# Pairwise bilinear products on one core: rows regrouped by partition, 102 stores over a ring of three, one transposed-x buffer, W in ten half loads

## The chip, the cores and the metric

The kernel runs on one core of a Trainium2 chip. Times are device microseconds, as medians of several executions; the span on a profile's page, from the first to the last instruction, is about 1.8 us shorter. Each kernel was compared with runs of the kernel before on the same chip.

## The reference, cut to what matters

```python
B, F, D = 4096, 32, 64                        # x: (B, F, D), W: (496, D, D), all float32
i_idx, j_idx = np.triu_indices(F, k=1)        # 496 pairs i < j
vi, vj = x[:, i_idx, :], x[:, j_idx, :]
inter = jnp.einsum('bpd,pde->bpe', vi, W) * vj
return inter.reshape(B, -1)                   # (4096, 31744): 520 MB
```

The output is 520 MB, against 42 MB of input. Below, a "unit" is one pair: 64 output columns. One tile is 128 batch rows and 496 units.

## The kernel before: the parts that matter

Two rows i of the triangle, 2p and 2p+1, run together: their two 64-row matmuls fill two PSUM banks, and one "doubled" multiply on VectorE takes both through an access pattern with two runs.

```python
STORES = [[0, 1], [2, 3], [4, 5], [6, 7, 8], [9, 10, 11, 12, 13, 14, 15]]
RING = 28160                                   # 440 units
def runs(tl, a, b, n):                         # two runs of n columns, at a and at b
    ap = tl[:, a : a + n]
    return bass.AP(ap.tensor, ap.offset, [list(ap.ap[0]), [b - a, 2], list(ap.ap[1])])
...
for p in range(NPR):                           # 16 loads of W, both halves at once
    nc.sync.dma_start(out=wp, in_=w[:, woff[p] : woff[p] + width[2 * p]])
...
for s, group in enumerate(STORES):             # five stores to a tile
    if at + store_w[s] > RING: at = 0
    osb = ring[:, at : at + store_w[s]]
    ...
            nc.vector.tensor_tensor(           # never leaves its own store's stretch
                runs(osb, o[0], o[1], n[0]), runs(pm, 0, half, n[0]),
                runs(xt, xj[0], xj[1], n[0]), ALU.mult)
    nc.sync.dma_start(out=out[ts(t, P), o0 : o0 + store_w[s]], in_=osb)
```

Of the kernel before, what the change touches and what calls it, by code (L numbers as in the profile page):

```python
# [1 line left out]

# [6 lines left out]

F32 = mybir.dt.float32  # L10
ALU = mybir.AluOpType

P = 128
BANK = 512
BANKS = 8
CHUNK = BANK

STORES = [[0, 1], [2, 3], [4, 5], [6, 7, 8], [9, 10, 11, 12, 13, 14, 15]]
PREFETCH_AT = [5, 6]
RING = 28160  # L20


@with_exitstack
def pair_bilinear_kernel(
    ctx: ExitStack,
    tc: tile.TileContext,
    x: bass.AP,
    w: bass.AP,
    out: bass.AP,
    F: int,  # L30
    D: int,
):




















    nc = tc.nc
    B = x.shape[0]
    NT = B // P
    NPR = F // 2

    width = [(F - 1 - i) * D for i in range(F)]
    off = [sum(width[:i]) for i in range(F)]
    woff = [sum(width[0 : 2 * p : 2]) for p in range(NPR)]  # L60
    store_w = [sum(width[2 * p] + width[2 * p + 1] for p in g) for g in STORES]

    const = ctx.enter_context(tc.tile_pool(name="const", bufs=1))
    xtpool = ctx.enter_context(tc.tile_pool(name="xT", bufs=2))
    psum = ctx.enter_context(tc.tile_pool(name="ps", bufs=1, space=bass.MemoryType.PSUM))

    ident = const.tile([P, P], F32, tag="ident", name="ident")
    make_identity(nc, ident)

    def runs(tl, a, b, n):  # L70

        ap = tl[:, a : a + n]
        return bass.AP(ap.tensor, ap.offset, [list(ap.ap[0]), [b - a, 2], list(ap.ap[1])])


    xbuf = [const.tile([P, (F + 1) * D], F32, tag=f"x{b}", name=f"x{b}") for b in range(2)]
    for xb in xbuf:
        nc.gpsimd.memset(xb[:, F * D :], 0.0)  # L78

    def load_x(t):  # L80
        xt = xbuf[t % 2]
        nc.scalar.dma_start(out=xt[:, : F * D], in_=x[ts(t, P), :])
        return xt

    pring = psum.tile([P, BANKS * BANK], F32, tag="pring", name="pring")
    bank = 0

    def take_banks(n):

        nonlocal bank  # L90
        if bank + n > BANKS:
            bank = 0
        got = pring[:, bank * BANK : (bank + n) * BANK]
        bank = (bank + n) % BANKS
        return got

    def transpose_x(xT, t, xt, g):

        n = 2 * BANK // P
        pt = take_banks(2)  # L100
        for c in range(n):
            nc.tensor.transpose(pt[:, ts(c, P)], xt[:, ts(n * g + c, P)], ident)  # L102
        nc.scalar.copy(xT[:, ts(g, 2 * BANK)], pt)  # L103

    def new_xT(t):
        return xtpool.tile([P, NPR * P], F32, tag="xT", name=f"xT_{t}")

    ring = const.tile([P, RING], F32, tag="ring", name="ring")
    at = 0
    xs = {0: load_x(0)}  # L110

    w_sb = []
    for p in range(NPR):
        wp = const.tile([P, width[2 * p]], F32, tag=f"w{p}", name=f"w{p}")
        nc.sync.dma_start(out=wp, in_=w[:, woff[p] : woff[p] + width[2 * p]])
        w_sb.append(wp)

    xTs = {0: new_xT(0)}
    for g in range(2):
        transpose_x(xTs[0], 0, xs[0], g)  # L120

    for t in range(NT):
        xt, xT = xs.pop(t), xTs.pop(t)
        if t + 1 < NT:
            xs[t + 1] = load_x(t + 1)
        for s, group in enumerate(STORES):
            if at + store_w[s] > RING:
                at = 0
            osb = ring[:, at : at + store_w[s]]
            at += store_w[s]  # L130
            o0 = off[2 * group[0]]
            for p in group:
                if t + 1 < NT and p in PREFETCH_AT:
                    if t + 1 not in xTs:
                        xTs[t + 1] = new_xT(t + 1)
                    transpose_x(xTs[t + 1], t + 1, xs[t + 1], PREFETCH_AT.index(p))
                for c0 in range(0, width[2 * p], CHUNK):
                    n = [max(0, min(CHUNK, width[2 * p + h] - c0)) for h in range(2)]
                    half = -(-n[0] // BANK) * BANK
                    pm = take_banks(2 * half // BANK)  # L140
                    for b0 in range(0, n[0], BANK):
                        b1 = min(b0 + BANK, n[0])
                        for h in range(2):
                            if b0 < n[h]:
                                nc.tensor.matmul(  # L145
                                    pm[:, h * half + b0 : h * half + b1],
                                    xT[h * D : (h + 1) * D, ts(p, P)],
                                    w_sb[p][h * D : (h + 1) * D, c0 + b0 : c0 + b1],
                                    start=True,
                                    stop=True,  # L150
                                )
                    o = [off[2 * p + h] - o0 + c0 for h in range(2)]
                    xj = [(2 * p + h + 1) * D + c0 for h in range(2)]
                    if n[1] > half - BANK and o[1] + n[0] <= store_w[s]:
                        nc.vector.tensor_tensor(  # L155
                            runs(osb, o[0], o[1], n[0]),
                            runs(pm, 0, half, n[0]),
                            runs(xt, xj[0], xj[1], n[0]),
                            ALU.mult,
                        )  # L160
                    else:
                        for h in range(2):
                            if n[h]:
                                nc.vector.tensor_tensor(  # L164
                                    osb[:, o[h] : o[h] + n[h]],
                                    pm[:, h * half : h * half + n[h]],
                                    xt[:, xj[h] : xj[h] + n[h]],
                                    ALU.mult,
                                )
            nc.sync.dma_start(out=out[ts(t, P), o0 : o0 + store_w[s]], in_=osb)  # L170


# [33 lines left out]
```

## Time and profile before

| | before |
|---|---|
| median, range | 1339.8 us, 1339.71 to 1339.87 |
| DMA queues, sum of the shares | 98.9% of 16 engines |
| VectorE, TensorE busy | 90%, 85% |
| first store's first packet, last completion | 27.6 us, 1336.8 us |

The main groups of instructions on the page (line, engine, operation, operands, count; busy us and mean ns; idle before and what ended it), and two lines of the list of DMA issues (size of each, median us from issue to landing):

```profile
L155 DVE TENSOR_TENSOR ring<-pring,x 128x1024 f32<-128x1024 f32 (+3 forms) x1056 | 1115.8, 1102 | 115.3 <-DMA out_dram<-ring 55.9
L145 PE MATMUL pring<-w,xT 64*128 64x512 f32 (+4 forms) x4864 | 1077.5, 560 | 165.7 <-DVE ring L155 161.4
...
out_dram<-ring SPq DMA_DIRECT2D x32, 3776.0 KB, 21.9
...
x<-in_x_dram ACTq DMA_DIRECT2D x32, 1024.0 KB, 14.2
```

A store lands 22 us after its issue although 3.8 MB take about 9 us at the measured rate: there is always another store ahead of it in the queue. That backlog is what keeps the DMA engines busy.

### The profile page before, as it was taken

How to read it: one execution, taken by the hardware profiler on the slowest of the kernel's cores; microseconds unless marked ns; L12 is line 12 of the kernel's file. 1: busy time of each engine (PE TensorE's matmuls, PEld its weight loads, DVE VectorE, ACT ScalarE, POOL GpSimd, SP SyncE). 2: the span in 40 equal slices, each digit the busy share in tenths (PEclk: the TensorE clock that was granted, in tenths of full speed). 3: DMA queues.
4: the chain of work that ended last, by engine and by line, in shares of the span. 5: the costliest groups of instructions: out<-in, count | busy, mean ns of one | idle time of the engine just before them, and what ended most of it. 6: DMA issues, size and time to landing. Idle time of an engine off the chain costs nothing.

```text
span 1338.1 us, 13157 instructions
## 1 busy us (share of the span) xinstructions
PE 1142.4 (85%) x5376; PEld 511.0 (38%) x5376; DVE 1199.8 (90%) x1376; ACT 66.1 (5%) x65; POOL 0.9 (0%) x8
## 2 busy tenths in 40 slices
PE   7899788898988988988889888889788898988982
PEld 3344333343344433433333334434344333433431
DVE  6999899898899988999889989899898998998993
ACT  1000000000000000000000000000000000000000
POOL 0000000000000000000000000000000000000000
PEclk9999999999998999999999999999999999999996
DMA  9999999999999999999999999999999999999996
GB/s 393 427 430 433 431 427 435 424 428 432 430 430 428 424 425 430 421 429 430 416 427 415 428 433 403 429 422 423 430 418 411 431 417 432 411 424 432 422 424 272
DMA packets 30012, 562.89 MB, mean 421 GB/s; under 512 B 3456, under 2 KB 3840, under 8 KB 5376
## 3 DMA queue, kind: packets, MB, share of 16 engines
q1 hardware_dynamic: 25344, 528.49, 92.7%
q10 hardware_dynamic: 4608, 33.56, 6.0%
q8 instruction: 42, 0.69, 0.2%
q14 instruction: 18, 0.15, 0.0%
HBM read 41.94 MB, written 520.09 MB: 420 GB/s over the span
## 4 chain that ended last, share of the span: by engine, by line
DMA 41%; DVE 39%; PE 16%; issue 2%; DVEq 0%
DMA out_dram<-ring 41%; DVE ring L155 35%; PE pring L145 13%; DVE ring L164 4%; PE pring L102 3%; DMA x<-in_x_dram 1%; DVEq L155 0%; DVEq L164 0%
## 5 line engine op out<-in xcount | busy, mean ns | idle before, releaser
L155 DVE TENSOR_TENSOR ring<-pring,x 128x1024 f32<-128x1024 f32 (+3 forms) x1056 | 1115.8, 1102 | 115.3 <-DMA out_dram<-ring 55.9
L145 PE MATMUL pring<-w,xT 64*128 64x512 f32 (+4 forms) x4864 | 1077.5, 560 | 165.7 <-DVE ring L155 161.4
L145 PEld LDWEIGHTS pring<-w,xT 64*128 64x128 f32 x4864 | 452.5, 189 | 758.6 <-DVE ring L155 601.3
L103 ACT COPY xT<-pring 128x1024 f32<-128x1024 f32 x64 | 64.8, 1013 | 1193.8 <-PE pring L102 1193.8
L164 DVE TENSOR_TENSOR ring<-pring,x 128x64 f32<-128x64 f32 (+3 forms) x320 | 114.5, 383 | 3.7 <-DVE ring L155 0.5
L102 PE MATMUL pring<-ident,x 128*128 128x128 f32 x512 | 73.6, 290 | 8.5 <-DMA x<-in_x_dram 8.5
L102 PEld LDWEIGHTS pring<-ident,x 128*128 128x128 f32 x512 | 58.5, 147 | 46.9 <-issue 36.9
L103 ACT ACT_TABLE_LOAD x1 | 1.3, 1283 | 1.7 <-PEq L198 1.7
masks.py:199 POOL TENSOR_SCALAR_AFFINE_SELECT ident<-ident 128x128 f32<-128x128 f32 x1 | 0.3, 294 | 0.0
L78 POOL MEMSET x<- 128x64 f32 x2 | 0.2, 152 | 0.0
masks.py:197 POOL MEMSET ident<- 128x128 f32 x1 | 0.2, 205 | 0.3 <-POOLq L198 0.3
L198 POOL MEMSET const-bfloat16-1.0<- 128x1 bf16 x1 | 0.1, 102 | 0.0
L198 POOL MEMSET const-uint8-127<- 128x1 uint8 x1 | 0.1, 102 | 0.0
L198 POOL MEMSET const-float32-0.0<- 128x1 f32 x1 | 0.1, 99 | 0.2 <-issue 0.2
L198 POOL MEMSET const-float32-1.0<- 128x1 f32 x1 | 0.1, 99 | 0.0
## 6 DMA issues: line engine op xcount, KB each, us to landing
out_dram<-ring SPq DMA_DIRECT2D x32, 3776.0 KB, 21.9
out_dram<-ring SPq DMA_DIRECT2D x32, 3264.0 KB, 21.6
out_dram<-ring SPq DMA_DIRECT2D x32, 3168.0 KB, 22.4
out_dram<-ring SPq DMA_DIRECT2D x32, 2912.0 KB, 21.4
out_dram<-ring SPq DMA_DIRECT2D x32, 2752.0 KB, 22.0
x<-in_x_dram ACTq DMA_DIRECT2D x32, 1024.0 KB, 14.2
w<-in_w_dram SPq DMA_DIRECT2D x1, 992.0 KB, 7.5
w<-in_w_dram SPq DMA_DIRECT2D x1, 928.0 KB, 11.8
```

The costliest lines, as they stand in the source:

```text
L78: nc.gpsimd.memset(xb[:, F * D :], 0.0)
L102: nc.tensor.transpose(pt[:, ts(c, P)], xt[:, ts(n * g + c, P)], ident)
L103: nc.scalar.copy(xT[:, ts(g, 2 * BANK)], pt)
L145: nc.tensor.matmul(pm[:, h * half + b0 : h * half + b1], xT[h * D : (h + 1) * D, ts(p, P)], w_sb[p][h * D : (h + 1) * D, c0 + b0 : c0 + b1 ...
L155: nc.vector.tensor_tensor(runs(osb, o[0], o[1], n[0]), runs(pm, 0, half, n[0]), runs(xt, xj[0], xj[1], n[0]), ALU.mult,)
L164: nc.vector.tensor_tensor(osb[:, o[h] : o[h] + n[h]], pm[:, h * half : h * half + n[h]], xt[:, xj[h] : xj[h] + n[h]], ALU.mult,)
L198: nc = bacc.Bacc("TRN2", target_bir_lowering=False, num_devices=1)
```

## The change

Its intent: each partition takes 32 neighbouring batch rows, so that a partition's output is one contiguous run and stores need not end with a tile. 101 stores of 157 units and a short one go through a ring of three slots, so fewer and longer packets. One transposed-x buffer pays for the larger ring. W is stored without padding and loaded by halves of 64 partitions.

```diff
-STORES = [[0, 1], [2, 3], [4, 5], [6, 7, 8], [9, 10, 11, 12, 13, 14, 15]]
-RING = 28160
+LOADS = [[0], [1], [2, 3], [4, 5, 6], [7, 8, 9, 10, 11, 12, 13, 14, 15]]
+STORE = 157 * 64
+SLOTS = 3
 ... (x of a tile: x[t], repacked on the host; out: (128, 32 * 31744))
-        nc.sync.dma_start(out=wp, in_=w[:, woff[p] : woff[p] + width[2 * p]])
+    for g in LOADS:
+        for h in range(2):
+            nc.sync.dma_start(out=w_sb[h * D : (h + 1) * D, a:b], in_=w[h * D : (h + 1) * D, a:b])
 ... (xT: one buffer, halves rewritten at pairs 9 and 3)
+                q = [t * cols + off[2 * p + h] + c0 for h in range(2)]
+                if n[1] and in_one_store(q[0], n[0]) and in_one_store(q[1], n[0]):
+                    at = [v % (SLOTS * STORE) for v in q]
+                    nc.vector.tensor_tensor(
+                        runs(ring, at[0], at[1], n[0]), runs(pm, 0, BANK, n[0]),
+                        runs(xt, xj[0], xj[1], n[0]), ALU.mult)
+                else:                          # single multiplies, cut at a store's end
+                    for h in range(2):
+                        multiply(q[h], pm, h * BANK, xt, xj[h], n[h])
+                if done // STORE * STORE > stored:
+                    store_to(done // STORE * STORE)
```

More of the change, by code (lines that the diff above doesn't have):

```diff
@@ L16 @@
 CHUNK = BANK
-STORES = [[0, 1], [2, 3], [4, 5], [6, 7, 8], [9, 10, 11, 12, 13, 14, 15]]
-PREFETCH_AT = [5, 6]
-RING = 28160
+LOADS = [[0], [1], [2, 3], [4, 5, 6], [7, 8, 9, 10, 11, 12, 13, 14, 15]]
+FIRST_HALF_AT, SECOND_HALF_AT = 9, 3
+STORE = 157 * 64
+SLOTS = 3
 @with_exitstack
@@ L53, in pair_bilinear_kernel @@
     nc = tc.nc
-    B = x.shape[0]
-    NT = B // P
+    NT = x.shape[0]
     NPR = F // 2
@@ L59, in pair_bilinear_kernel @@
     off = [sum(width[:i]) for i in range(F)]
-    woff = [sum(width[0 : 2 * p : 2]) for p in range(NPR)]
-    store_w = [sum(width[2 * p] + width[2 * p + 1] for p in g) for g in STORES]
+    cols = sum(width)
+    woff = [sum(width[i % 2 : i : 2]) for i in range(F)]
     const = ctx.enter_context(tc.tile_pool(name="const", bufs=1))
-    xtpool = ctx.enter_context(tc.tile_pool(name="xT", bufs=2))
     psum = ctx.enter_context(tc.tile_pool(name="ps", bufs=1, space=bass.MemoryType.PSUM))
@@ L81, in load_x @@
         xt = xbuf[t % 2]
-        nc.scalar.dma_start(out=xt[:, : F * D], in_=x[ts(t, P), :])
+        nc.scalar.dma_start(out=xt[:, : F * D], in_=x[t])
         return xt
@@ L95, in take_banks, with transpose_x @@
         return got
-    def transpose_x(xT, t, xt, g):
+    xT = const.tile([P, NPR * P], F32, tag="xT", name="xT")
+    def transpose_x(xt, g):
         n = 2 * BANK // P
@@ L103, in transpose_x @@
         nc.scalar.copy(xT[:, ts(g, 2 * BANK)], pt)
-    def new_xT(t):
-        return xtpool.tile([P, NPR * P], F32, tag="xT", name=f"xT_{t}")
-    ring = const.tile([P, RING], F32, tag="ring", name="ring")
-    at = 0
-    xs = {0: load_x(0)}
-    w_sb = []
-    for p in range(NPR):
-        wp = const.tile([P, width[2 * p]], F32, tag=f"w{p}", name=f"w{p}")
-        nc.sync.dma_start(out=wp, in_=w[:, woff[p] : woff[p] + width[2 * p]])
-        w_sb.append(wp)
-    xTs = {0: new_xT(0)}
-    for g in range(2):
-        transpose_x(xTs[0], 0, xs[0], g)
+    ring = const.tile([P, SLOTS * STORE], F32, tag="ring", name="ring")
@@ new lines, in pair_bilinear_kernel, with store_to, in_one_store, multiply @@
+    stored = 0
+    def store_to(end):
+        nonlocal stored
+        at = stored % (SLOTS * STORE)
+        nc.sync.dma_start(out=out[:, stored:end], in_=ring[:, at : at + end - stored])
+        stored = end
+    def in_one_store(q, n):
+        return q // STORE == (q + n - 1) // STORE
+    def multiply(q, pm, c, xt, xj, n):
+        while n:
+            m = min(n, STORE - q % STORE)
+            at = q % (SLOTS * STORE)
+            nc.vector.tensor_tensor(
+                ring[:, at : at + m], pm[:, c : c + m], xt[:, xj : xj + m], ALU.mult
+            )
+            q, c, xj, n = q + m, c + m, xj + m, n - m
@@ L122, in pair_bilinear_kernel @@
+    xs = {0: load_x(0)}
+    w_sb = const.tile([P, woff[F - 2] + width[F - 2]], F32, tag="w", name="w")
+    for g in LOADS:
+        for h in range(2):
+            a = woff[2 * g[0] + h]
+            b = woff[2 * g[-1] + h] + width[2 * g[-1] + h]
+            if h and g is LOADS[-1]:
+                b += D
+            nc.sync.dma_start(
+                out=w_sb[h * D : (h + 1) * D, a:b], in_=w[h * D : (h + 1) * D, a:b]
+            )
+    transpose_x(xs[0], 0)
     for t in range(NT):
-        xt, xT = xs.pop(t), xTs.pop(t)
+        xt = xs.pop(t)
@@ L124, in pair_bilinear_kernel @@
         if t + 1 < NT:
             xs[t + 1] = load_x(t + 1)
-        for s, group in enumerate(STORES):
-            if at + store_w[s] > RING:
-                at = 0
-            osb = ring[:, at : at + store_w[s]]
-            at += store_w[s]
-            o0 = off[2 * group[0]]
-            for p in group:
-                if t + 1 < NT and p in PREFETCH_AT:
-                    if t + 1 not in xTs:
-                        xTs[t + 1] = new_xT(t + 1)
-                    transpose_x(xTs[t + 1], t + 1, xs[t + 1], PREFETCH_AT.index(p))
-                for c0 in range(0, width[2 * p], CHUNK):
-                    n = [max(0, min(CHUNK, width[2 * p + h] - c0)) for h in range(2)]
-                    half = -(-n[0] // BANK) * BANK
-                    pm = take_banks(2 * half // BANK)
-                    for b0 in range(0, n[0], BANK):
-                        b1 = min(b0 + BANK, n[0])
-                        for h in range(2):
-                            if b0 < n[h]:
-                                nc.tensor.matmul(
-                                    pm[:, h * half + b0 : h * half + b1],
-                                    xT[h * D : (h + 1) * D, ts(p, P)],
-                                    w_sb[p][h * D : (h + 1) * D, c0 + b0 : c0 + b1],
-                                    start=True,
-                                    stop=True,
-                                )
-                    o = [off[2 * p + h] - o0 + c0 for h in range(2)]
-                    xj = [(2 * p + h + 1) * D + c0 for h in range(2)]
-                    if n[1] > half - BANK and o[1] + n[0] <= store_w[s]:
-                        nc.vector.tensor_tensor(
-                            runs(osb, o[0], o[1], n[0]),
-                            runs(pm, 0, half, n[0]),
-                            runs(xt, xj[0], xj[1], n[0]),
-                            ALU.mult,
-                        )
-                    else:
-                        for h in range(2):
-                            if n[h]:
-                                nc.vector.tensor_tensor(
-                                    osb[:, o[h] : o[h] + n[h]],
-                                    pm[:, h * half : h * half + n[h]],
-                                    xt[:, xj[h] : xj[h] + n[h]],
-                                    ALU.mult,
-                                )
-            nc.sync.dma_start(out=out[ts(t, P), o0 : o0 + store_w[s]], in_=osb)
@@ new lines, in pair_bilinear_kernel @@
+        for p in range(NPR):
+            if p == SECOND_HALF_AT:
+                transpose_x(xt, 1)
+            if p == FIRST_HALF_AT and t + 1 < NT:
+                transpose_x(xs[t + 1], 0)
+            for c0 in range(0, width[2 * p], BANK):
+                n = [max(0, min(BANK, width[2 * p + h] - c0)) for h in range(2)]
+                pm = take_banks(2)
+                for h in range(2):
+                    if n[h]:
+                        a = woff[2 * p + h] + c0
+                        nc.tensor.matmul(
+                            pm[:, h * BANK : h * BANK + n[0]],
+                            xT[h * D : (h + 1) * D, ts(p, P)],
+                            w_sb[h * D : (h + 1) * D, a : a + n[0]],
+                            start=True,
+                            stop=True,
+                        )
+                q = [t * cols + off[2 * p + h] + c0 for h in range(2)]
+                xj = [(2 * p + h + 1) * D + c0 for h in range(2)]
+                if n[1] and in_one_store(q[0], n[0]) and in_one_store(q[1], n[0]):
+                    at = [v % (SLOTS * STORE) for v in q]
+                    nc.vector.tensor_tensor(
+                        runs(ring, at[0], at[1], n[0]),
+                        runs(pm, 0, BANK, n[0]),
+                        runs(xt, xj[0], xj[1], n[0]),
+                        ALU.mult,
+                    )
+                else:
+                    for h in range(2):
+                        multiply(q[h], pm, h * BANK, xt, xj[h], n[h])
+                done = q[0] + n[0] if c0 + BANK < width[2 * p] else q[1] + n[1]
+                if done // STORE * STORE > stored:
+                    store_to(done // STORE * STORE)
@@ L173 @@
+    if stored < NT * cols:
+        store_to(NT * cols)
 def kernel(r_inputs, L0_rec_W):
@@ L179 @@
     NP = L0_rec_W.shape[0]
-    x = np.ascontiguousarray(r_inputs).reshape(B, F * D)
+    NT = B // P
+    x = np.ascontiguousarray(r_inputs.reshape(P, NT, F * D).transpose(1, 0, 2))
     wt = np.transpose(L0_rec_W, (1, 0, 2))
@@ L185 @@
     first = [sum(n[:i]) for i in range(F)]
-    halves = [
-        np.concatenate(
-            [
-                np.pad(wt[:, first[i] : first[i] + n[i]], ((0, 0), (0, h), (0, 0)))
-                for i in range(h, F, 2)
-            ],
-            axis=1,
-        )
-        for h in range(2)
-    ]
-    w = np.ascontiguousarray(np.stack(halves)).reshape(2 * D, -1)
+    w = np.zeros((2, D, sum(n[0::2]), D), wt.dtype)
+    for h in range(2):
+        of_h = [wt[:, first[i] : first[i] + n[i]] for i in range(h, F, 2)]
+        w[h, :, : sum(n[h::2])] = np.concatenate(of_h, axis=1)
+    w = w.reshape(2 * D, -1)
     nc = bacc.Bacc("TRN2", target_bir_lowering=False, num_devices=1)
@@ L200 @@
     w_d = nc.dram_tensor("in_w_dram", w.shape, F32, kind="ExternalInput").ap()
-    o_d = nc.dram_tensor("out_0_dram", (B, NP * D), F32, kind="ExternalOutput").ap()
+    o_d = nc.dram_tensor("out_0_dram", (P, NT * NP * D), F32, kind="ExternalOutput").ap()
     with tile.TileContext(nc) as tc:
@@ L204 @@
     r = run_bass_kernel_spmd(nc, [{"in_x_dram": x, "in_w_dram": w}], core_ids=[0])
-    return r.results[0]["out_0_dram"]
+    return r.results[0]["out_0_dram"].reshape(B, NP * D)
```

## The prediction

> **What bounds the kernel now.** I read the head of the page first (engine shares, the slices), then the DMA queues, the chain that ended last, the waits of VectorE, and last the transfers stretch by stretch.
>
> ```profile
> PE 1142.4 (85%) x5376; PEld 511.0 (38%) x5376; DVE 1199.8 (90%) x1376; ACT 66.1 (5%) x65; POOL 0.9 (0%) x8
> ...
> DMA  9999999999999999999999999999999999999996
> ...
> DMA packets 30012, 562.89 MB, mean 421 GB/s; under 512 B 3456, under 2 KB 3840, under 8 KB 5376
> ...
> q1 hardware_dynamic: 25344, 528.49, 92.7%
> q10 hardware_dynamic: 4608, 33.56, 6.0%
> q8 instruction: 42, 0.69, 0.2%
> ...
> DMA 41%; DVE 39%; PE 16%; issue 2%; DVEq 0%
> ```
>
> VectorE is busy 90% of the span, but the sixteen DMA engines are busy in every slice but the last. The queue shares add up to 98.9%: 0.989 x 1338.1 = 1323 us of packets on the mean DMA engine. Nothing else comes near. The chain of waits gives VectorE 39% because it counts the work between two waits for a freed ring; that is no sign that VectorE is short. Its waits:
>
> ```profile
> DVE ring L155 <- DMA out_dram<-ring: 55.9, 35, 3.0
> DVE ring L155 <- PE pring L145: 30.7, 27, 12.9
> ```
>
> Thirty-five times it stands until a store has left the ring. It could work faster than the stores drain. By stretch (columns: PE, PEld, DVE, ACT, POOL, granted clock, DMA share, GB/s):
>
> ```profile
> 0.00:26.00 26.00, 16.73 (x76) 8.62 (x77) 12.90 (x14) 3.31 (x3) 0.88 (x8) 1.00 0.94 377
> 26.00:80.00 54.00, 49.46 (x244) 22.40 (x243) 52.59 (x61) 4.05 (x4) 0.00 (x0) 1.00 1.02 433
> 80.00:160.00 80.00, 70.11 (x340) 31.11 (x338) 74.59 (x86) 4.05 (x4) 0.00 (x0) 1.00 1.00 431
> 160.00:640.00 480.00, 415.02 (x1952) 187.04 (x1950) 438.50 (x504) 22.28 (x22) 0.00 (x0) 0.97 1.00 428
> 640.00:1280.00 640.00, 559.64 (x2640) 249.11 (x2640) 586.11 (x674) 32.41 (x32) 0.00 (x0) 0.97 0.99 422
> 1280.00:1320.00 40.00, 31.44 (x134) 12.74 (x132) 35.11 (x41) 0.00 (x0) 0.00 (x0) 0.94 0.98 417
> 1320.00:1326.00 6.00, 0.00 (x0) 0.00 (x0) 0.00 (x0) 0.00 (x0) 0.00 (x0) 0.50 1.02 436
> 1326.00:1338.00 12.00, 0.00 (x0) 0.00 (x0) 0.00 (x0) 0.00 (x0) 0.00 (x0) 0.50 0.06 26
> ```
>
> Two things are to be seen. The transfers run at 431 to 433 GB/s at first and at 422 later. And in the last 12 us the share is 0.06, one engine of sixteen. In the trace's packet records fifteen engines post their last completion between 1326.6 and 1326.9 us, the sixteenth at 1336.8. While the others run, that one's packets take 2 to 3% longer than the median (888 ns for 23,296 bytes against 865; alone at the end it also does 865). Nearly one sixteenth of all store packets are longer by such an amount. I read this as one slow DMA engine: by mid-run it is about 10 us behind, the ring holds the other fifteen to its pace, and its own sum of packets is what the time consists of. This reading from packet records is the least certain part of the diagnosis; the DMA bound itself is certain.
>
> [...]
>
> **The change part by part.**
> What a packet costs: medians are 309 ns for 8,192 bytes and 1119 ns for 30,208, so (1119 - 309) / 22,016 = 0.0368 ns per byte (27.2 bytes per ns) and 7.6 ns fixed. A completion packet is 9 ns.
>
> Stores. The bytes are the same, 520.09 MB. A row of a store was 21.5 to 29.5 KB, is now 157 x 256 = 40,192 bytes. Stores fall from 160 to 102, packets per engine at 8 each from 1280 to 816: 464 x 7.6 ns = 3.5 us, and 58 completions x 9 ns = 0.5 us. Together -4.0 us, on the path as each engine's packets are the path.
>
> Ring. Before, 440 units of 64 columns in which stores of 118, 102, 86, 99 and 91 wrapped with waste; now three slots of 157, 471 units. VectorE fills a slot in some 157/496 of its 37.5 us per tile (1199.8/32), 11.9 us, and the DMA drains one in 157/496 of 41 us, 13.0 us. When a slot comes free two others are still queued, 26 us of work, so the slow engine never starves. It doesn't starve now either, so this buys nothing unless the waits cost the slow engine something.
>
> W. 16 loads of 128 partitions become ten of 64, alternately lower and upper half. Bytes: 31,808 columns x 64 rows x 4 = 8.14 MB instead of 8.39; 0.25 MB / 16 / 27.2 = 0.6 us, and 88 fewer packets per engine (16 x 8 to 10 x 4) another 0.7: -1.3 us. [...]508.9 KB per engine goes at 13.6 bytes per ns, 37.4 us, not 18.7: +18.7 us. These loads lie ahead of the first store in the same queue. Before, that store's first packet moves at 27.6 us: 1.75 of start, about 21 us of W packets, 5 of two x loads. [...] This loss isn't recovered, as the DMA has no slack later. VectorE, fed by W at half rate (16,384 bytes per unit at 217.5 GB/s are 0.0753 us, and VectorE needs 37.5/496 = 0.0756), still has the first 157 units at about 26 us and the second slot at 39, so at 45 there is work queued and no gap.
>
> VectorE. I counted instructions by shape: 1376 become 1458: 701 doubled ones of 1024 elements in place of 768, and more singles where a store ends inside a chunk. With the durations by shape (1024: 1178 ns busy each, 896: 1082, 640: 820, 384: 551, singles of 64: 218 to 512: about 683, worked out from 448: 616 and 384: 549) the sum is about 1274 against 1254 worked out in the same way: +20 us, to about 1220 of busy time. 91% of the span, in the shadow of the DMA: 0.
>
> TensorE. The same 2432 matmul and 512 transpose calls, reordered; the single transposed-x buffer has its first half rewritten at pair 9 and its second at pair 3, when its readers are past: 0. At the start only eight transposes stand ahead of the first matmul: about 0.5 us earlier, hidden behind W.
>
> Sum: -4.0 - 1.3 + 18.7 = +13.4 us on 1339.8 = 1353.2. Since the half rate is no fact of this trace[...], I take about 3 us off: 1350.
>
> **The rivals.**
> First, W's loads run at full rate, because lower and upper loads overlap in the queue. [...] The time would be 1339.8 - 5.3 = 1334.5.
> Second, the larger slots and equal stores free the fifteen engines from the slow one. For it: 422 against 431 GB/s. Against: the one that ends last is the slow one, which the ring doesn't hold up. If its slowness came from the addresses of the old layout and went, the rate of 431 throughout would save 552 MB x (1/421 - 1/431), about 30 us: 1305 to 1325 by what W costs.
> Third, the new output pitch, 32 x 124 KiB = 3968 KiB, is close to 4 MiB. [...] If it came true at 10%, the time would be beyond 1440.
> Fourth, VectorE becomes the bound through its 82 extra instructions and coarser slots. Against: 11.9 of 13.0 us per slot. At worst a few us.
>
> **Range and chances.** Most of the weight is at 1344 to 1356 (W at half or nearly half rate), a fifth at 1330 to 1340, little elsewhere. Eight in ten: 1330 to 1360. Faster by 2% means under 1313: only the second rival, with W cheap: 0.05. Slower by 2% means over 1366.6: the third, or a worse W: 0.08. Within 2%: 0.87.
>
> **What would show it.** The W loads should land at some 43 to 46 us, not 26, with about 220 GB/s in the stretch after the x loads; the first store should begin there. W packets should take about twice their bytes at 27.2 per ns. A store packet of 40,192 bytes should take 1486 ns. VectorE busy should be near 1220 us with waits for the stores, the DMA share near 1.00 at 422 to 430 GB/s from 50 us on, and one engine about 10 us late at the end. I am wrong if W lands by 30 us, if steady GB/s leave 420 to 432, if store packets take clearly more than 1486 ns, or if DMA gaps appear between stores.

The marked cuts are passages that no trace or run of this case shows: a section of general figures and the reasons given for W's half rate and for the 3 us taken off, then the arguments for and against the first and the third rival. The sum: -4.0 - 1.3 + 18.7 = +13.4 us on 1339.8 gave 1353.2, and 3 us off gave 1350. But its largest term, +18.7 us, stood under an "if": it assumed that loads over 64 partitions move at half of the 27.2 bytes per ns that the medians gave (13.6; for sixteen engines the 217.5 GB/s in the text). No trace before the change showed that; the one after does, with 1575 ns for a W packet of 20,736 bytes, 13.2 bytes per ns. Also cut is the estimate for the first store's first packet, 26 us at the full rate and some 45 at half; it moved at 46.2 us. In the third rival, "it" is that the new pitch costs time.

## The result, and the profile after

The changed kernel takes 1424.12 us (1423.46 to 1425.52, 5 runs) against 1339.80 (1339.70 to 1339.98, 5 runs): ratio 1.0631, 95% interval 1.0617 to 1.0646. It is slower by 84 us. The predicted 1350 and its range of 1330 to 1360 miss it.

The page after: busy times, the DMA slices, packets, and the two queues that carry the data.

```profile
PE 1180.9 (83%) x5376; PEld 533.1 (37%) x5376; DVE 1212.5 (85%) x1458; ACT 66.1 (5%) x65; POOL 0.9 (0%) x8
...
DMA  9999999989998979999789999998989999989899
...
DMA packets 20157, 562.64 MB, mean 396 GB/s; under 512 B 2304, under 2 KB 2304, under 8 KB 2688
...
q1 hardware_dynamic: 15488, 528.24, 88.4%
q10 hardware_dynamic: 4608, 33.56, 6.3%
```

The bytes are the same but for 0.25 MB of W, the packets a third fewer, but the slices are no longer all nines: the queues' shares add up to 94.9% with the 0.2% of instruction fetches, not 98.9%. By stretch (columns as in the prediction):

```profile
0.00:26.00 26.00, 12.56 (x38) 6.08 (x38) 8.15 (x7) 2.29 (x2) 0.88 (x8) 1.00 0.95 230
26.00:46.00 20.00, 18.36 (x76) 10.09 (x76) 16.50 (x19) 1.01 (x1) 0.00 (x0) 0.91 1.01 213
46.00:80.00 34.00, 29.94 (x136) 16.07 (x136) 28.38 (x35) 2.02 (x2) 0.00 (x0) 0.90 1.00 427
80.00:160.00 80.00, 63.89 (x269) 29.26 (x268) 61.37 (x76) 3.04 (x3) 0.00 (x0) 0.89 0.93 392
160.00:640.00 480.00, 412.87 (x1925) 181.73 (x1921) 432.30 (x520) 23.28 (x23) 0.00 (x0) 0.97 0.96 407
640.00:1280.00 640.00, 535.58 (x2448) 242.63 (x2446) 551.48 (x664) 29.36 (x29) 0.00 (x0) 0.93 0.94 397
```

Two separate losses are to be seen. Up to 46 us the engines are busy (share 0.95 to 1.01) but move only 213 to 230 GB/s: the loads of W, as predicted. From 80 us on the rate divided by the share is 421 to 424 GB/s, little less than before, but 4 to 7% of the engines' time is empty: that was not predicted. VectorE's waits say with what it goes together (us in total, times, longest):

```profile
DVE ring L174 <- DMA out_dram<-ring: 116.1, 15, 12.9
DVE ring L174 <- PE pring L163: 39.1, 30, 17.0
```

Before there were 35 waits for a store, of 3.0 us at most. Now there are 15, of up to 12.9 us. One of them, in VectorE's timeline (start, duration, instructions, idle time ahead and its releaser):

```profile
103.72 1.22 DVE L174 TENSOR_TENSOR ring<-pring,x 128x1024 f32<-128x1024 f32 x1 [1.23 <-PE pring L163]
110.77 1.82 DVE L174 TENSOR_TENSOR ring<-pring,x 128x384 f32<-128x384 f32 x2 [5.83 <-DMA out_dram<-ring]
```

and the DMA around it:

```profile
104.00:108.00 4.00, 2.02 (x2) 0.45 (x2) 0.94 (x1) 0.00 (x0) 0.00 (x0) 0.63 1.02 436
108.00:111.00 3.00, 0.00 (x0) 0.00 (x0) 0.23 (x1) 0.00 (x0) 0.00 (x0) 0.50 0.13 54
111.00:114.00 3.00, 2.61 (x10) 1.86 (x12) 2.58 (x4) 0.00 (x0) 0.00 (x0) 0.50 1.00 429
```

The doubled multiply at 110.77 finishes the sixth store, in the third slot, and its second half lies in the seventh, in the first slot. The only store still to land then was the fifth, in the middle slot, which this multiply does not touch. It landed at 110.68 by the trace's landing records. So VectorE waited for the store that had been issued last. When that landed, nothing was queued behind it, and all sixteen engines ran dry until the sixth store was issued at 111.36. The trace's record of this multiply names the semaphore that it waits for, number 101: it is the fifth store's, which raised it sixteen times in the landing records, the last at 110.68. The wait also stands in the built program, where it can be read without a chip.

In the packet records there are 17 moments after 50 us at which no engine moves anything for over 0.2 us, 43 us in all; before there is none. The theory (A), a guess: for a pattern of two runs, the waits are placed for the whole range from the lowest to the highest address. Across the ring's end that is the whole ring. Going through the loop's indices by hand, 33 doubled multiplies lie across it, in 21 of the ring's 33 turns. The trace agrees for 15 turns: each of the 15 waits in the line above ends when the newest store lands, 116.1 us in all. In the other six turns there is no such wait; the twelfth store, for one, was issued at 191.4 us, before the eleventh, in the middle slot, had landed at 195.7. So the whole range is not always taken, and theory A is too strong as it stands. In those six the two runs lie 444, 450 or 456 units apart, which three divides, and in the 15 it does not; why that should matter is open. Rivals: (B) three slots of 157 units are too coarse in themselves; (C) the new output pitch is slow.

### The profile page after: what moved, and what is told of

The parts are those of the page before. It is cut to its first block, busy times and chain, and to the rows that moved or that the text cites. A ratio compares the mean times of both kernels' runs of the same rounds, so it can differ in the third digit from the quotient of the medians.

```text
span 1422.3 us, 13143 instructions
## 1 busy us (share of the span) xinstructions
PE 1180.9 (83%) x5376; PEld 533.1 (37%) x5376; DVE 1212.5 (85%) x1458; ACT 66.1 (5%) x65; POOL 0.9 (0%) x8
## 3 DMA queue, kind: packets, MB, share of 16 engines
q10 hardware_dynamic: 4608, 33.56, 6.3%
## 5 line engine op out<-in xcount | busy, mean ns | idle before, releaser
L163 PE MATMUL pring<-w,xT 64*128 64x512 f32 (+4 forms) x4864 | 1111.6, 567 | 192.0 <-DVE ring L174 171.4
L174 DVE TENSOR_TENSOR ring<-pring,x 128x1024 f32<-128x1024 f32 (+3 forms) x1062 | 1099.7, 1079 | 185.1 <-DMA out_dram<-ring 116.1
L163 PEld LDWEIGHTS pring<-w,xT 64*128 64x128 f32 x4864 | 476.2, 193 | 807.3 <-DVE ring L174 612.9
L130 DVE TENSOR_TENSOR ring<-pring,x 128x64 f32<-128x64 f32 (+7 forms) x396 | 138.3, 391 | 9.2 <-PE pring L163 2.9
## 6 DMA issues: line engine op xcount, KB each, us to landing
w<-in_w_dram SPq DMA_DIRECT2D x1, 1296.0 KB, 27.6
w<-in_w_dram SPq DMA_DIRECT2D x1, 832.0 KB, 19.6
```

What stands on the lines that cost most here:

```text
L130: nc.vector.tensor_tensor(ring[:, at : at + m], pm[:, c : c + m], xt[:, xj : xj + m], ALU.mult)
L163: nc.tensor.matmul(pm[:, h * BANK : h * BANK + n[0]], xT[h * D : (h + 1) * D, ts(p, P)], w_sb[h * D : (h + 1) * D, a : a + n[0]], start=Tr ...
L174: nc.vector.tensor_tensor(runs(ring, at[0], at[1], n[0]), runs(pm, 0, BANK, n[0]), runs(xt, xj[0], xj[1], n[0]), ALU.mult,)
```

## The experiments

### 1. Single multiplies across the ring's end

```diff
-if n[1] and in_one_store(q[0], n[0]) and in_one_store(q[1], n[0]):
+if n[1] and at[0] < at[1] and in_one_store(q[0], n[0]) and in_one_store(q[1], n[0]):
```

> The changed kernel, with a doubled multiply whose first half lies in the last slot and whose second half lies in the first slot of the ring split into two single ones (33 of them). Theory A (its range over the ring is taken to cover the middle slot too, so it waits for the store that was issued last, and all DMA engines run dry): the gaps go, about 1353 us, DMA share near 1.00 at 420 to 430 GB/s after the loads of W. Rival B (three slots of 157 are too coarse) or C (the new output pitch): it stays at 1415 to 1425.

Measured: 1356.94 us (1356.48 to 1357.76), ratio to before 1.0129. 67 us are gone with 33 multiplies split in two. Its stretches, and VectorE's waits for stores:

```profile
80.00:160.00 80.00, 72.29 (x329) 32.15 (x328) 74.01 (x94) 4.05 (x4) 0.00 (x0) 0.98 1.00 432
160.00:640.00 480.00, 429.06 (x1968) 187.63 (x1966) 443.44 (x546) 23.28 (x23) 0.00 (x0) 0.99 1.00 427
640.00:1280.00 640.00, 573.99 (x2620) 252.05 (x2618) 593.22 (x728) 31.38 (x31) 0.00 (x0) 0.99 1.00 423
```

```profile
DVE ring L130 <- DMA out_dram<-ring: 24.8, 30, 2.3
DVE ring L174 <- DMA out_dram<-ring: 23.2, 15, 2.6
```

The share is back at 1.00, the longest wait is 2.6 us in place of 12.9, no wait for the newest store is left, and the packet records have no dry moment. The queues' shares, worked out per engine, say it too: 94.9% of 1422.3 us left 73 us idle, 99.2% of 1356.0 leaves 11. Pitch, slots and packets are those of the changed kernel, so B and C fall as explanations of the 67 us. The waits at the ring's end are the cause; the rule by which they are placed is not shown. The 17 us above 1339.8 remain.

### 2. The same, split in the first half of the tiles only

```diff
+if n[1] and (at[0] < at[1] or t >= NT // 2) and in_one_store(...) ...
```

> The changed kernel with the doubled multiplies across the ring's end split in the first 16 tiles only; 17 of 33 stay, in 12 of 21 turns of the ring. If each such turn costs the same, 67 us x 12/21 = 38 us stay: about 1395 us, with DMA share near 1.00 up to about 660 us and near 0.94 after.

Measured: 1394.46 us (1393.45 to 1396.12), 37.5 us above the full split for 12 turns, 9 of which have the wait for the newest store in the trace: 4.2 us a wait. With all 21 turns it was 67.2 us for 15 waits, 4.5 each. The cost counts with the waits, roughly. Its profile shows the border between the two halves:

```profile
60.00:660.00 600.00, 538.32 (x2460) 236.86 (x2460) 555.73 (x688) 29.35 (x29) 0.00 (x0) 0.99 1.00 428
660.00:1380.00 720.00, 598.38 (x2748) 267.81 (x2746) 622.22 (x751) 32.39 (x32) 0.00 (x0) 0.94 0.94 396
```

### 3. Still doubled, but the lower address first

Across the ring's end the pattern's step is negative. To tell the sign from the range, the halves were swapped in all three operands.

```diff
+u, v = (0, 1) if at[0] < at[1] else (1, 0)
-runs(ring, at[0], at[1], n[0]), runs(pm, 0, BANK, n[0]), runs(xt, xj[0], xj[1], n[0])
+runs(ring, at[u], at[v], n[0]), runs(pm, u * BANK, v * BANK, n[0]), runs(xt, xj[u], xj[v], n[0])
```

> The changed kernel, where the doubled multiplies across the ring's end stay doubled but name the half with the lower address first, so that their step is positive. If what counts is the range from the first slot to the last, the waits stay: 1424 us within 5. If the negative step was the cause (a slow form, or a range taken wrongly for it alone), it falls to about 1357 us, as with the split.

Measured: 1424.77 us (1423.04 to 1424.94). The waits stand as before:

```profile
DVE ring L175 <- DMA out_dram<-ring: 114.3, 16, 12.6
```

It isn't the negative step: 15 waits for the newest store stand in the same turns as before. What lies between the two runs is left, with the six turns still unexplained.

### 4. W in loads of 128 partitions, with the split

```diff
-for h in range(2):
-    nc.sync.dma_start(out=w_sb[h * D : (h + 1) * D, a:b], in_=w[h * D : (h + 1) * D, a:b])
+nc.sync.dma_start(out=w_sb[:, a:b], in_=w[:, a:b])     # five loads, padding included
```

> The same split, and W in five loads of 128 partitions in place of ten of 64 (8.39 MB again). [...]18 to 19 us less than the run with the split alone: about 1335 us under theory A. If the loads of W were not on the path, no difference between the two.

Measured: 1338.90 us (1338.68 to 1339.02), ratio to before 0.9993 (0.9978 to 1.0008). That is 18.0 us less than with the split alone, as expected if loads over 64 partitions move at half rate. It is also 4 us more than the 1335 that the sum gave. Its page, to set beside the prediction's lines for the kernel before:

```profile
q1 hardware_dynamic: 15408, 528.49, 92.4%
q10 hardware_dynamic: 4608, 33.56, 6.5%
```

By the packet records SyncE's queue (q1: W and the stores) takes 1235.9 us an engine in place of 1240.5, the 4.6 us saved that the sum had. But the same x packets (q10) take 86.3 us in place of 79.8, 336 ns in the mean in place of 310.

### 5. The kernel before, W in halves

```diff
-nc.sync.dma_start(out=wp, in_=w[:, woff[p] : woff[p] + width[2 * p]])
+for h in range(2):
+    nc.sync.dma_start(out=wp[h * D : (h + 1) * D], in_=w[h * D : (h + 1) * D, woff[p] : ...])
```

> The kernel before, with each of its 16 loads of W cut into a lower and an upper half of 64 partitions, same bytes, same packets. Half rate on the path: 1339.8 + 19.3 = 1359 us. Not on the path, or full rate: 1340 us.

Measured: 1359.37 us (1358.86 to 1359.77): +19.6 us where 19.3 were expected. The first store's first packet moved at 47.2 us, not 27.6.

### 6. The changed kernel, only W in 128 partitions

The edit of experiment 4 without the split.

> The changed kernel with only the loads of W put back to 128 partitions, the doubled multiplies across the ring's end kept. If the two costs add up, 1424 - 19 = 1405 us; if the waits at the ring's end hide the late start, 1415 to 1424 us.

Measured: 1407.05 us (1405.32 to 1407.49), 17.1 us below the changed kernel. The two costs add up; the dry moments do not hide the late start.

### 7. The new rows alone

```diff
 # the kernel before, five stores to a tile
-nc.sync.dma_start(out=out[ts(t, P), o0 : o0 + store_w[s]], in_=osb)
+nc.sync.dma_start(out=out[:, t * cols + o0 : t * cols + o0 + store_w[s]], in_=osb)
 # and x[t] in place of x[ts(t, P), :], repacked on the host
```

> The kernel before with the new placing of the rows alone: partition p takes 32 neighbouring batch rows, output rows 3968 KiB apart in place of 124 KiB, everything else as before. If the pitch costs nothing: 1339.8 us within 1. If it takes back the 3 us that the fewer packets were to save: 1342 to 1344 us. If it were behind the 84 us, 1400 us or more.

Measured: 1339.78 us (1339.58 to 1339.97), ratio 0.9999 (0.9986 to 1.0013). The pitch of 3968 KiB costs nothing.

### 8. Four times the packets

To see whether the fixed cost of a packet is on the path, the kernel before stored each stretch in quarters.

```diff
-nc.sync.dma_start(out=out[...], in_=osb)
+dst, src = [v.rearrange("p (a c b) -> p c a b", a=2, c=2) for v in (out[...], osb)]
+for k in range(2):
+    nc.sync.dma_start(out=dst[:, k], in_=src[:, k])
```

> The kernel before, with every store cut into packets of a quarter of a row (two stores of two runs each), so 5120 store packets per DMA engine in place of 1280, same bytes and same places. If 7.6 ns fixed per packet lie on the path: 3840 x 7.6 ns = 29 us, and 160 more completions x 9 ns = 1.4 us: about 1370 us. If the pace of the last engine hides them: 1340 to 1345 us. The predicted saving of 4 us from fewer packets stands or falls with it.

Measured: 1387.57 us (1386.84 to 1388.25): +47.8 us. Less 1.4 for the completions, 46.4 us / 3840 packets = 12.1 ns each, more than the 7.6 ns that the prediction had worked out from the medians of a load's and a store's packet. So the cost is real and on the path, in this direction at least.

### 9. A first store that is ready in time

In experiment 4 the first store began at 28.7 us, a microsecond after W's last packet. Here it is cut into 118 and 39 units.

```diff
+if stored == 0 and done >= off[4]:
+    store_to(off[4])
```

> The run with the split and W in 128 partitions, with the first store issued in two pieces of 118 and 39 units, so that it is ready when W has landed. It started at 28.7 us there against W's end at 27.6, and the stretch from 26 to 80 us moved 417 GB/s against 433 before. If that late start ate the 2 to 3 us missing of the predicted gain of 4 us from fewer packets: 1336 to 1337 us. If the larger stores gain nothing anyway: 1338.9 us.

Measured: 1338.57 us (1337.72 to 1338.63), ratio to before 0.9989 (0.9975 to 1.0003). It started at 27.5 us, but only 0.3 us came of it.

### 10. Four slots of 118 units

`STORE = 118 * 64`, `SLOTS = 4`, on the kernel of experiment 4.

> The run with the split and W in 128 partitions, with four slots of 118 units (472 in all) in place of three of 157 (471): 135 stores. Packets rise by 264 per DMA engine, +2 us at 7.6 ns, +3 at 12. If three coarse slots cost what is missing of the 4 us from fewer packets (late first store included), 1336 to 1338 us; if they cost nothing, 1340 to 1342 us.

Measured: 1339.27 us (1339.07 to 1339.56), ratio 0.9998 (0.9984 to 1.0011). That lies between what was expected if coarse slots cost nothing (1340 to 1342) and if they cost what is missing (1336 to 1338): they may cost a microsecond or two, and this run doesn't settle it.

### 11 and 12. One DMA engine left out of some loads

The prediction read the pace as that of one slow DMA engine. Every third load of x went as 120 and 8 partitions, in the hope that 120 rows use fifteen engines and that the sixteenth is the slow one.

```diff
+if t % 3 == 0:
+    nc.scalar.dma_start(out=xt[:120, ...], in_=x[t * P : t * P + 120, :])
+    nc.scalar.dma_start(out=xt[120:, ...], in_=x[t * P + 120 : (t + 1) * P, :])
```

In the kernel before:

> The kernel before, with every third load of x (11 of 32) sent as 120 and 8 partitions in place of 128. If the prediction's reading is right that one slow DMA engine sets the pace, and if 120 rows go over 15 engines without that one, it has 11 x 2.5 = 27 us less to do: the 10 us between the last two completions at the end shrink below 4 us and the time falls by 5 to 20 us. If there is no such engine, or it is among the 15, 1338 to 1342 us.

In the kernel of experiment 9:

> The short first store together with every third load of x in 120 and 8 partitions. If one slow DMA engine sets the pace and is left out of the 120 rows: 5 to 20 us less than the run with the short first store. If not, the same time within 2 us.

Measured: 1348.60 us (1347.77 to 1348.93) and 1347.50 us (1346.98 to 1347.68), both 9 us worse. The 77 packets more (4685 against 4608) are what fifteen engines and eight would give. In the first, one engine still posts its last completion 9.9 us after most others (1344.5 against 1334.6 us). If it is the engine that lagged before, it was not relieved. Which one it is stays open, as the trace doesn't number the engines, and so does why it lags.

## Why the prediction was wrong, point by point

**The bound.** Right: the DMA queues bound the kernel before, and every split version ends within 1.3 us of it once W is loaded as before (the x loads left whole).

**W.** Right in rate and size; what causes the half rate is not shown. The sum had +18.7 us less the bytes and packets saved; the runs show 18.0 (experiments 1 and 4), 19.6 (5) and 17.1 (6). The W packet of 20,736 bytes took 1575 ns in the mean, against 771 worked out at full rate. The last load landed at 48.0 us, a little after the 43 to 46. The transfers moved 213 GB/s from 26 to 46 us, against 427 from 46 to 80 us, once the stores had begun. Nothing of the 3 us taken off is seen.

**The ring.** This is the step that failed, and 67 of the 74 us between 1350 and 1424 are in it; the other 7 are the 3 us taken off and the 4 us of packets, below. The prediction said: "When a slot comes free two others are still queued, 26 us of work, so the slow engine never starves." That holds for the data's real dependencies. In 15 turns VectorE did not wait for the slot that it wrote; it waited for the store in the middle slot, the last one queued. The backlog was then 0, not 26 us. 1424.1 - 1356.9 = 67.2 us belong to that. That "DMA gaps appear between stores" stood in the list of what would prove it wrong, but no rival named a cause for them, and the prediction does not look at the multiplies' waits, which the built program shows without a chip.

**Packets.** The saving of 4.0 us did not reach the time. With the split, 1356.9 came against the sum's 1353.2. Experiment 4 against before should give 4.0 + 0.7 for W's fewer packets; it gave 0.9. The queue of W and the stores did save 4.6 us, so that term was sized well; the sum left out that the x packets would get longer, by 6.5 us an engine. Packets of one engine can overlap in the records (shares above 1.00, as the 1.02 from 26 to 80 us before), so this is the likely place of the missing 3 to 4 us and no proof. Larger packets are hardly the reason, as experiment 8 with its small ones has 336 ns too; it stays open. The pitch (7) takes no part, the late first store 0.3 us (9), the coarse slots perhaps a little (10).

**VectorE and TensorE.** Right: 1212.5 us of busy time where 1220 were expected, and nothing of it on the path in the split versions. Store packets took 1486 ns in the median, as worked out.

**The rivals.** First (W at full rate): refuted. Second (freeing the engines from the slow one): nothing of it is seen, 423 GB/s late in experiment 1 against 422. Third (pitch): refuted. Fourth (coarse slots): nearest in place, but its mechanism is refuted by experiment 1, which keeps the slots. The slow engine is supported as far as the traces go: in the kernel before, a store's last completion trails its eighth by 1.6 us at 39 us, 8.8 us at 408 us and 9 to 14 us from then on, and one engine is 8 to 10 us late at the end. That it sets the pace is not shown (experiments 11 and 12). In the changed kernel it is 1.2 us late (1421.1 against 1419.9), as in each dry moment all engines ran empty.

**Is there a version that beats both?** Clearly better than the changed kernel: the split with W in 128 partitions, and a first store in two pieces, 1338.57 us. Its interval against the kernel before reaches 1.0003, so that one isn't beaten.

## What to carry to other kernels

When an instruction names two places of a ring, look at where the waits are placed, not only at the places: a pattern across the ring's end may be made to wait for what lies between, as in 15 turns of 21 here. A store-bound kernel lives on its backlog, so each wait for the newest store cost a full stop, 4.5 us here (67.2 us for 15), though VectorE had 9% to spare. And loads over 64 partitions took twice as long (1575 ns a packet against 771 worked out), which cost 17.1 to 19.6 us because the queue behind them had no slack.
